# A later place for the router's products, and an earlier one for norms without a partner, in a two-layer graph-attention and mixture-of-experts kernel

## The chip, the cores and the metric

The kernel runs on one core of a Trainium2 chip. A core has a matrix engine (TensorE, PE in the profile, with its weight loads as PEld), a vector engine (VectorE, DVE), a scalar engine (ScalarE, ACT), a general engine (GpSimd, POOL) and an engine that only issues transfers and waits (SyncE, SP). Each takes its own instructions in their written order and waits for others by semaphores. The metric is the device time of one execution in microseconds, the median of several runs.

## The reference

The input x has 64 batches of 256 tokens with 256 features, and a mask of 256 x 256 says which tokens may attend to which. Cut to what matters:

```python
# layer 0
x = x + elu(attention(layernorm(x), adj, W0, a0, heads=4))
x = x + layernorm(x) @ Wf.T + bf
# layer 1
x = x + relu(attention(layernorm(x), adj, W1, a1, heads=1))
t = layernorm(x)                       # 16384 tokens
logits = t @ router.T                  # 8 experts
two best experts per token, weights by softmax over the two
x = x + t + sum over the two: weight * (gelu(t @ w1[e] + b1[e]) @ w2[e] + b2[e])
```

`attention` forms q = h @ W, adds one score per source token and one per target token, applies a leaky relu and the mask, takes a softmax over the targets and multiplies with q. Each batch needs four layer norms: of the input (x0), after the first attention (x1), after the linear layer (x2) and after the second attention (x2 again). Everything is float32.

## The kernel before, in words

**One batch.** `batch_layers` (L506) is a generator that writes the instructions of one batch up to the next `yield`. Its main steps, with the lines that the profile names: the input is turned (L116) and normed, q is projected (L405), scores are spread and masked (L475 on PE, L482 on DVE), the first values are multiplied (L496, 32 products of 65 columns), divided and passed through elu (L503, L534 or L539, L545 to L549); the linear layer (transposes L389, copy L395, products L560, L566 on DVE); the second projection (L440, then L447 to L453 on ACT), second scores (L459, L464) and second values (L496 again, 8 products of 257 columns, reciprocals L503, L582 on ACT, L586 on DVE); the last norm's factors (L591, L594), the normed rows (L600) and the base of the output (L605); and last the router (transposes L389, copy L395, eight small products L630, and a copy of the logits on DVE, L634).

**Norms.** `norm_stats` (L362) takes mean and variance on DVE (L374, L375). The power -1/2 is taken on POOL (L382 adds epsilon, L383 takes the power). To save POOL instructions the power is taken for two norms at once: the first norm of a step is noted in `half_done`, and the second one in the same step calls `finish_norms` (L380) for both. A norm that finds no partner in its step is finished by itself at the end of that step. In full operation two norms meet in each step that has any. Toward the end, when no new batch starts, four of them have no partner: two x1 norms, whose factor L566 uses, and two last norms, whose factor L591 uses.

**Experts.** The tokens of most batches (62 of 64) are sorted by expert. `route` (L939) finds places for the rows of a chunk of batches (the last two chunks have one batch each, the six before them two), and `send` (L920) writes the rows to a buffer `xs` in device memory with indirect DMAs that POOL issues (L922). `expert_pair` (L742) handles 256 rows of one expert: SP loads the rows (L758, L769) and the expert's weights (L784), DVE turns the rows, PE multiplies (L816, gelu on ACT L822, L831), DVE adds a bias (L841), ACT weights them (L809), and `scatter` (L846) adds them to the output with two indirect DMAs from POOL (L852). A scatter waits until the pair of scatters before it has landed, since both may add to the same row. A load of rows waits until the rows sent before it have landed. After the last chunk, SP fills the ends of the experts' regions (L1024), and loads after that wait for it. The last two batches are computed through all experts instead (`dense_expert`, L868).

**Order.** The order is written by a small scheduler (L1090 to L1128). In each step every active generator is advanced once, by rank from low to high; the rank is the number that it yielded last. A new batch starts every third step. So all that is yielded with 35 in a step is written before what is yielded with 40, and so on; sends have 95 and scatters 97. Ranks that matter here: the router's products 35 (L626), the second values 40 (L577), the last norms before the others 60 (L585). Whatever this order says, each engine follows; nothing is reordered later except by waits. PSUM (eight banks) is shared by all these steps, each result taking one bank until it has been read.

The first 16 batches (`EARLY`, L639, `early` at L530) already differ a little: some of their work on DVE is given to ACT and POOL.

The softmax here doesn't subtract the row's maximum and nothing guards it: scores larger than these inputs give would overflow.

## Time and profile before

| | us |
|---|---|
| median of 3 runs | 1607.51 (1606.32 to 1608.09) |
| the profiled execution's own time | 1611.36 |
| its span, first to last instruction | 1609.5 |
| busy: PE | 1468.2 (91%) |
| busy: weight loads | 1299.9 (81%) |
| busy: DVE | 1308.6 (81%) |
| busy: ACT | 860.2 (53%) |
| busy: POOL | 914.6 (57%) |
| mean granted TensorE clock | 0.963 of full speed |

Four stages can be told apart by time. Up to about 320 us there is little expert work yet, and DVE is the busiest (256 of 284 us from 76 to 360). From there to about 1340 us PE is full. From 1340 to 1426 us the last batches pass through and no engine is full. From 1426 to 1552 PE works off the remaining experts, and a chain of scatters follows up to 1609.

In the lines that follow, a group or an instruction is given by time, engine, source line, what is written and read, and in brackets the idle time of its engine before it with what ended that. `rstd` is the factor of a norm, `mv` its mean and variance, `pl` the logits, `pv` the values, `xr` the rows of an expert's pair, `we` its weights.

### The profile page before, as it was taken

The page shows a single profiled execution, that of the slowest core. Times are in us where ns is not written, and L with a number is a line of the kernel's source. Part 1 is how long each engine was busy: PE and PEld are TensorE (multiplying, and loading weights), DVE is VectorE, ACT ScalarE, POOL GpSimd, SP SyncE. Part 2 cuts the span into 40 slices and gives each one's busy share as a digit, 9 for nine tenths or more (in the row PEclk, how much of TensorE's full clock was granted, in tenths as well). Part 3 has the DMA queues.
Part 4 walks back from the last instruction along what each step waited for, and adds up shares of the span by engine and source line. Part 5 has one row for each costly group of instructions (what it writes and reads, how often), then busy time and mean ns, then how long its engine had stood idle before and what let it go on. Part 6 is the DMA issues. An engine that isn't in the chain of part 4 may idle for free.

```text
span 1609.5 us, 30304 instructions
## 1 busy us (share of the span) xinstructions
PE 1468.2 (91%) x8474; PEld 1299.9 (81%) x8474; DVE 1308.6 (81%) x4431; ACT 860.2 (53%) x1968; POOL 914.6 (57%) x875
## 2 busy tenths in 40 slices
PE   7998988999999999999999999999999999489960
PEld 5887777888888888888888888888888887468850
DVE  6898988999898989898989899899899987545530
ACT  2455455465666666556666665555556655343320
POOL 2332636265757576666657575756665567733444
PEclk9999998999999999999999999999999999799985
DMA  5712223466666666665657576664766566787733
GB/s 156 207 50 57 83 74 90 113 152 131 134 145 135 141 143 133 149 145 126 156 119 152 130 155 126 159 129 108 155 129 152 131 120 134 185 174 152 133 47 45
DMA packets 364134, 207.39 MB, mean 129 GB/s; under 512 B 264248, under 2 KB 334912, under 8 KB 363968
## 3 DMA queue, kind: packets, MB, share of 16 engines
q1 hardware_dynamic: 313344, 137.07, 34.7%
q0 software_dynamic: 49632, 67.39, 23.0%
q8 instruction: 70, 1.15, 0.3%
q10 hardware_dynamic: 992, 0.99, 0.2%
q14 instruction: 96, 0.79, 0.2%
HBM read 116.19 MB, written 89.15 MB: 128 GB/s over the span
## 4 chain that ended last, share of the span: by engine, by line
PE 70%; DVE 17%; DMA 3%; ACT 3%; issue 3%; POOL 2%; SPq 1%; DVEq 0%; POOLq 0%; ACTq 0%
PE pv L496 16%; PE ph L816 14%; PE py L831 14%; PE pq L405 6%; PE pq L440 6%; PE pf L560 5%; PE pt L389 4%; DVE z L482 3%; DVE stats L374 2%; PE pl L630 2%; ACT xT L395 2%; DMA out_dram<-y,xt 2%; POOL out_dram L852 1%; DVE mv L375 1%; PE pd L475 1%
## 5 line engine op out<-in xcount | busy, mean ns | idle before, releaser
L852 POOL DMA_INDIRECT out_dram<-y,xt x262 | 417.0, 1592 | 199.7 <-issue 51.1
L496 PE MATMUL pv<-q,z 128*128 128x65 f32 (+1 forms) x2560 | 370.3, 300 | 1.3 <-DVE z L482 1.3
L496 PEld LDWEIGHTS pv<-q,z 128*128 128x128 f32 x2560 | 331.5, 194 | 13.8 <-DVE z L482 1.4
L922 POOL DMA_INDIRECT xs<-xng,pos x248 | 251.2, 1013 | 66.4 <-issue 63.7
L382 POOL TENSOR_SCALAR rstd<-mv 128x4 f32<-128x4 f32 (+1 forms) x132 | 59.3, 449 | 395.5 <-DVE mv L375 347.5
L831 PE MATMUL py<-w2s,hT 128*128 (+1 forms) x1176 | 266.5, 380 | 1.2 <-ACT hT L822 1.2
L395 ACT COPY xT<-pt 128x512 f32<-128x512 f32 x192 | 113.7, 592 | 276.3 <-PE pt L389 276.3
L816 PE MATMUL ph<-sT,we 128*128 128x256 f32 x1048 | 243.6, 386 | 10.0 <-DMA we<-wpack 7.8
L831 PEld LDWEIGHTS py<-w2s,hT 128*128 128x128 f32 x1176 | 219.9, 191 | 30.0 <-ACT hT L822 2.0
L816 PEld LDWEIGHTS ph<-sT,we 128*128 128x128 f32 x1048 | 199.2, 194 | 37.2 <-issue 8.2
L482 DVE SCALAR_TENSOR_TENSOR z<-pd,q,mask 128x256 f32<-128x256 f32 x512 | 211.1, 474 | 0.9 <-PE pd L475 0.9
L822 ACT ACTIVATE hT<-ph,we 128x256 f32<-128x256 f32 x294 | 122.4, 472 | 152.9 <-PE ph L816 130.9
L383 POOL TENSOR_TENSOR rstd<-rstd,mhalf 128x4 f32<-128x4 f32 (+1 forms) x132 | 162.7, 1233 | 11.0
L374 DVE BATCH_NORM_STATS2 stats<-x 128x6 f32<-128x256 f32 x384 | 156.2, 407 | 2.2
L809 ACT ACTIVATE y<-y,w 128x256 f32<-128x256 f32 x262 | 112.4, 501 | 76.0 <-DVE y L841 75.5
L440 PE MATMUL pq<-wx,xT 128*128 128x259 f32 x512 | 130.1, 397 | 18.6 <-ACT xT L395 14.9
L405 PE MATMUL pq<-wx,xT 128*128 128x268 f32 x512 | 133.9, 407 | 5.6 <-DVE xT L116 3.7
L841 DVE TENSOR_TENSOR y<-py,b2s 128x512 f32<-128x512 f32 x131 | 85.9, 685 | 57.9 <-PE py L831 52.6
L440 PEld LDWEIGHTS pq<-wx,xT 128*128 128x128 f32 x512 | 92.5, 190 | 45.2 <-ACT xT L395 29.7
L560 PE MATMUL pf<-wfT,xT 128*128 128x256 f32 x512 | 122.8, 383 | 0.1
L405 PEld LDWEIGHTS pq<-wx,xT 128*128 128x128 f32 x512 | 99.0, 198 | 25.1 <-issue 3.2
L375 DVE BATCH_NORM_AGGREGATE mv<-stats 128x2 f32<-128x6 f32 x512 | 93.1, 182 | 17.5
(156 smaller groups left out, 2262.3 us busy)
## 6 DMA issues: line engine op xcount, KB each, us to landing
we<-wpack SPq DMA_DIRECT2D x139, 288.0 KB
xr<-xs SPq DMA_DIRECT2D x524, 64.0 KB
xblk<-in_x_dram SPq DMA_DIRECT2D x256, 64.0 KB
xin<-in_x_dram SPq DMA_DIRECT2D x64, 256.0 KB
out_dram<-base SPq DMA_DIRECT2D x64, 256.0 KB
out_dram<-y,xt POOLq DMA_INDIRECT x262, 4.1
xs<-xng,pos POOLq DMA_INDIRECT x248, 2.7
xs<-fill SPq DMA_DIRECT2D x9, 260.0 KB
```

The lines of the kernel that those rows point to most:

```text
L374: nc.vector.bn_stats(stats[:, t, :], src[:, t, :])
L383: nc.gpsimd.tensor_tensor(rstd[:, :n], rstd[:, :n], mhalf[:, :n], ALU.pow)
L395: nc.scalar.copy(dst, pt)
L405: nc.tensor.matmul(pq.rearrange("p h c -> p (h c)"), xT[:, k, t * P : (t + 1) * P], wx[:, k, :], start=(k == 0), stop=(k == KT - 1),)
L440: nc.tensor.matmul(pq, xT[:, k, t * P : (t + 1) * P], wx1[:, k, :], start=(k == 0), stop=(k == KT - 1),)
L482: nc.vector.scalar_tensor_tensor(z[:, j, :], pd[:, i, :], q[:, j, h, d + 2 : d + 3], mask[:, j, :], op0=ALU.max, op1=ALU.mult,)
L496: nc.tensor.matmul(pv[:, h, :], z[:, j, t * P : (t + 1) * P], q[:, j, h, : d + 1], start=(j == 0), stop=(j == NT - 1),)
L560: nc.tensor.matmul(pf[:, t, :], xT[:, k, t * P : (t + 1) * P], wfT[:, k, :], start=(k == 0), stop=(k == KT - 1),)
L816: nc.tensor.matmul(ph[:, f, :], we[:, k * D + f * P : k * D + (f + 1) * P], xT[:, k, :], start=(k == 0), stop=(k == KT - 1),)
L831: nc.tensor.matmul(py[:, t, :], hT[:, f, t * P : (t + 1) * P], w2s[:, e, f * D : (f + 1) * D].rearrange("p e c -> p (e c)"), start=(f == 0 ...
L852: d = nc.gpsimd.indirect_dma_start(out=out_rows, out_offset=bass.IndirectOffsetOnAxis(ap=xt[:, t, 0:1].bitcast(I32), axis=0), in_=y[:, t, ...
L922: d = nc.gpsimd.indirect_dma_start(out=xs_d[: E * CAP * PAIR, :], out_offset=bass.IndirectOffsetOnAxis(ap=at, axis=0), in_=xe, in_offset=None,
```

## The change

Two edits in the order; no instruction is added or taken away.

```diff
@@ batch_layers
         xT = transposed(xe[:, :, :D], *(("xTd", DENSE) if dense else ()), blocks=True)
-        yield 35
+        yield 45 if early else 35
         pl = bank("pl", [NT, E])
@@ the scheduler's step
             while queue:
                 *_, entry = heapq.heappop(queue)
+                if half_done and entry[0] > 75:
+                    finish_norms(NT)
                 entry[0] = next(entry[2], None)
```

The first edit gives the router's products of batches 0 to 15 the rank 45, so that they are written behind the second values of another batch (rank 40) where they stood ahead of them. On PE the eight L630 products change places with eight L496 products of 257 columns; on DVE the copy of the logits (L634) goes behind two reciprocals (L503). The banks of the three results change hands accordingly: the second half of the next first projection (L405), which took the router's bank before and does so after, waits for the copy of the logits either way.

The second edit finishes a norm that has no partner before the first entry of a rank above 75 in its step, and no longer at the step's end. Where nothing of such a rank is issued by POOL in that step, the order on POOL stays. It changes in four places, all toward the end: the norms at 1318.3, 1343.4, 1373.2 and 1397.9 us of the profile. The first two move ahead of two sends and two scatters, the third ahead of two sends and two scatters, the fourth ahead of two scatters. All other instructions of POOL keep their order, and so do those of ACT and SP.

## The prediction

> **What bounds the kernel now.** I read the stages first (busy time by stretch of time: length, then busy us of PE, weight loads, DVE, ACT, POOL, then granted clock, DMA share, GB/s).

> ```profile
> 1240.00:1300.00 60.00, 59.52 (x351) 53.48 (x350) 54.70 (x200) 34.50 (x75) 36.03 (x33) 1.00 0.59 122
> 1340.00:1375.00 35.00, 24.78 (x117) 20.38 (x115) 20.07 (x108) 13.71 (x31) 25.36 (x24) 0.90 0.68 125
> 1375.00:1400.00 25.00, 14.10 (x64) 12.25 (x64) 13.55 (x75) 10.36 (x21) 16.95 (x16) 0.77 0.67 134
> 1400.00:1426.00 26.00, 15.51 (x61) 12.63 (x61) 17.40 (x75) 11.78 (x25) 13.32 (x11) 0.76 0.87 219
> 1426.00:1552.00 126.00, 124.82 (x568) 108.90 (x569) 61.08 (x146) 49.84 (x113) 52.46 (x34) 0.99 0.71 135
> ```

> The long middle (320 to 1340 us) is full on PE and the change doesn't touch its order. From 1340 to 1426 nothing is full: that stage is a chain of waits, and half of the change lies there. The other half lies before about 345 us (batches 0 to 15), where DVE is busy over 90% of the time.

> In the tail I read who DVE waits for (1300 to 1426 us; total, times, longest), then SP's DMA queue (1340 to 1430):

> ```profile
> DVE by L591 <- POOL rstd L383: 18.1, 3, 10.1
> DVE x L566 <- POOL rstd L383: 9.0, 2, 6.4
> ```
> ```profile
> SPq L758 <- DMA xs<-xng,pos: 25.6, 3, 13.0
> ```

> Four norms without a partner hold DVE for 2.60, 6.38, 7.81 and 10.11 us, 26.9 in sum. But SP, which issues the loads that the last experts need, is held by something else: sent rows that must land. POOL in order of time shows why:

> ```profile
> 1340.42 1.61 POOL L852 DMA_INDIRECT out_dram<-y,xt  x1 [0.35 <-issue]
> 1342.34 1.57 POOL L852 DMA_INDIRECT out_dram<-y,xt  x1 [0.30 <-ACT hT L822]
> 1343.38 0.82 POOL L382 TENSOR_SCALAR rstd<-mv 128x2 f32<-128x2 f32 x1
> ...
> 1347.09 0.23 POOL L382 TENSOR_SCALAR rstd<-mv 128x4 f32<-128x4 f32 x1 [2.07 <-DVE tail L679]
> 1347.40 1.02 POOL L383 TENSOR_TENSOR rstd<-rstd,mhalf 128x4 f32<-128x4 f32 x1
> 1348.61 1.62 POOL L852 DMA_INDIRECT out_dram<-y,xt  x1 [0.19 <-issue]
> ...
> 1370.27 1.60 POOL L852 DMA_INDIRECT out_dram<-y,xt  x1 [1.54 <-issue]
> ...
> 1385.43 1.00 POOL L922 DMA_INDIRECT xs<-xng,pos  x1 [0.30 <-issue]
> ```
> ```profile
> 1388.19 1.98 SPq L758 DMA_DIRECT2D xr<-xs  x4
> ...
> 1400.13 7.00 SPq L1024 DMA_DIRECT2D xs<-fill  x8
> 1412.45 1.92 SPq L758 DMA_DIRECT2D xr<-xs  x4
> ```

> The send at 1385.43 plus 2.7 us (median of the sends to landing here) is 1388.1, and there SP's 13.0 us wait ends. From then on SP issues without a pause, except 5.0 us for the landing of the fill, until the weight loads at 1422, whose landing starts PE's last full stretch at 1425.87; that one ends at 1552, and a chain of scatters follows to the end. So the tail's path is POOL, then SP, and not the engine with the longest waits.

> **The change part by part.** The sum is made against the profiled execution, 1611.36 us (span 1609.5), and the difference is put on the median 1607.51, which is 3.85 lower.

> *Norm A (was 1318.3 to 1319.9).* It comes ahead of the sends at 1312.55. Its statistics were complete at 1310.25, so it doesn't stand. A lone norm costs POOL 1.1 us (scatter's end 1343.91 to rstd's end 1345.0), so two sends and two scatters go 1.1 later, the scatters' end to 1319.9. DVE's wait of 2.60 goes, the next paired norm's statistics are there at 1319.3 instead of 1321.9, and that norm (1.3 to 2.1 us) ends by 1322.0 instead of 1324.2. What follows on POOL is 2.2 earlier.

> *Norm B (was 1343.9 to 1345.0).* Its statistics were complete at 1329.4. With A's shift the scatter that ended at 1337.40 ends at 1335.2; B adds 1.1, so sends and scatters behind it are 1.1 earlier and end at 1342.8. DVE's 6.38 goes: it reaches L566 at 1338.7, the next paired norm no longer waits until 1347.09 but runs 1342.8 to 1344.2. What is late next is the scatter of 1348.61: it must wait until the scatter before has landed. Seven such gaps between 1308 and 1396 (end of one pair to start of the next) are 3.05 to 4.67, mean 3.65. 1342.8 + 3.65 = 1346.5: 2.1 earlier (ends 2.7 and 1.1). The scatters of 1356.14, 1362.67 and 1370.27 each waited for that landing already (4.02, 3.05, 4.15), so the 2.1 is handed on unchanged.

> *Norm C (was 1373.7 to 1374.8).* It goes ahead of the sends at 1366.42, which fit: they end 1.3 later, at 1370.0, inside the idle 1.54 before 1370.27. It leaves the line between the scatter's end at 1373.73 and the send at 1375.01: 1.28. Now 3.4 earlier, through the serial run of sends and scatters to the send of 1385.43, hence SP's loads and the last PE stretch. DVE's 7.81 mostly goes; its cover is that SP waits for the sends anyway.

> *Norm D (was 1397.9 to 1399.6).* It goes ahead of a scatter pair that waits 4.67 for landing, where it costs nothing. The four sends behind come 1.3 earlier, but SP's load of 1412.45 waits for the fill, not for them. 10.11 us of DVE's wait goes for nothing.

> SP itself and its waits keep their order. On POOL no instruction is added; the four norms only change places. Tail: 3.4 us gain.

> *Router behind the second values, 16 batches.* Eight products (0.96 to 1.06 us) go behind eight of L496 (1.84). PE stood before the router in 7 batches, for 8.2 us together, the longest

> ```profile
> 178.81 1.06 PE L630 MATMUL pl<-rT,xT 128*128 128x8 f32 x8 [2.34 <-ACT xT L395]
> 252.31 1.88 PE L630 MATMUL pl<-rT,xT 128*128 128x8 f32 x8 [2.26 <-ACT xT L395]
> ```

> and the values, ready long before (z ended at 248.7 in the second), now fill it. But who is paid? DVE carries the chain from 145 to 320, and of its waits there

> ```profile
> DVE rinv L503 <- PE pv L496: 3.5, 3, 1.6
> DVE x L566 <- PE pf L560: 0.7, 3, 0.3
> ```

> two of 1.6 follow PE's wait in the routing (L956), which stays. What the swap can end is 0.33 at 257.85 and 0.16 at 95.94: 0.5 us. Upper bound: all DVE waits for PE from 76 to 330 us, 5.6. Lower: DVE's copy of the logits comes after two reciprocals (0.22 for both), and the second half of the next L405 products takes its bank: 16 x 0.22 = 3.5 lost if PE always stood there; it stood at L405 for DVE's reciprocal once, 1.3. I take 0.5, as PE has slack in that stage.

> In that wait the granted clock fell: 1.00 in 248 to 252, 0.52 in 252 to 256, and eight L496 products took 3.77 instead of 1.98. [...]

> [...] The row: the power took 0.72 with DVE idle, 1.52 at 1322.68 with DVE busy. By that A and B cost 0.8 more each, and the tail would gain 1.8 instead of 3.4.

> Sum: 3.4 + 0.5 = 3.9. 1607.5 - 3.9 = **1603.6 us**.

> **The rivals.**
> *B, POOL gives it back.* The sends wait behind the norms (1.1 each for A and B), the power is slow beside DVE, and the paired norms come no earlier on POOL because sends and scatters are ahead of them. For: POOL is serial from 1366 to 1388. Against: paired norms are late through DVE's wait. Only C's 1.28 and part of 0.5 remain: about 1606.
> *C, more goes through.* DVE, ACT and PE run ahead, base stores clear sooner, and four landings (after 1342.8, 1352, 1359.6, 1366) all take the shortest, 3.05: 0.6 + 1.0 + 1.1 = 2.7 more, 6.6 in all: 1600.9.
> *D, slower.* The same four landings lengthen, because loads and base stores now bunch with them: their forecast sum is 14.9; at 4.7 each (seen once: 4.67) the gain is gone, at 6.0 each it is 24.0, a loss of 9.1 - 3.9 = 5.2: 1612.7. It decides above 4.7 mean. Against: DMA's share is already 0.67 in these windows and the mean was 3.65.

> **How the numbers follow.** 0.2%, 3.2 us, is about what a measurement of this kernel tells from no change. Forecast 0.50, own range 2.6 to 5.5 gain (1602.0 to 1604.9), of which 0.36 counts as faster and 0.14 as same, since 3.9 stands just past the bound; B 0.22, same; C 0.15, faster; D 0.13, slower. Faster 0.51, same 0.36, slower 0.13. Range: from a little below C, 1600, to 1609, short of D; some 0.18 lies outside.

> **What would show it.** Right: DVE's waits for lone rstd gone (under 4 us of 26.9 left); the scatter of 1348.61 at about 1346.5; SP's load of 1388.19 at about 1385; PE's last full stretch from about 1422.5, unchanged in length; PE's waits before the router under 2 us, with DVE's end of the early stage within 1 us. Wrong: SP's load at 1388 or later (B, D); landing gaps above 4.7 (D); SP waiting for something other than sends, or the early stage 3 us or more shorter, since then PE carried it and not DVE.

## The result: slower by 0.4%, and the profile after

The changed kernel took 1612.48 us (median of 7 runs, 1611.37 to 1614.87) where the kernel before, run beside it, took 1606.32 (7 runs, 1602.15 to 1608.09). The ratio is 1.0039, with a 95% interval from 1.0026 to 1.0051: 6.2 us slower, between 4.2 and 8.2. I had forecast 3.9 us faster, with 1609.0 as the upper end.

The two profiled executions differ by much less, 1612.47 against 1611.36 us, because the profile of before happens to lie above all timed runs of before. To see where time went, I set each instruction of DVE against the same instruction of the other profile. In the first 60 us, where nothing is changed, the changed kernel came out 3.7 us ahead by chance. From 60 to 370 us it lost 5.4 us. From there to 1290 us the distance kept within 0.3 us. From 1290 to 1500 us it gained 0.6. The loss came in three jumps: about 1.5 us at 140 us, 2.4 at 287 and 1.4 at 326; the first two stand behind a routing. So the loss lies in the early stage, where edit 1 (the router) is, and the gain of edit 2 (the norms) is small.

What DVE waits for PE in the early stage, 76 to 330 us, in the profile after (total, times, longest):

```profile
DVE rinv L503 <- PE pv L496: 6.7, 5, 1.6
DVE z L464 <- PE pd L459: 2.3, 3, 0.8
```

Before, the same two rows had 3.5 (shown in the prediction) and 0.8. That is 4.7 us more of waiting on the engine that carries this stage. Why PE was late is seen in PE's own waits in that stretch, first before:

```profile
PE pp L956 <- DVE m L948: 8.5, 3, 3.7
PE pl L630 <- ACT xT L395: 8.2, 7, 2.3
```

and after:

```profile
PE pp L956 <- DVE m L948: 14.0, 3, 5.4
PE pl L630 <- ACT xT L395: 2.8, 4, 0.8
```

The two rows add up to 16.7 us before and 16.8 after. The edit did end most of PE's waits at the router, as forecast, but the idle time wasn't removed. It went to the next place where PE has to wait for DVE: the routing products (L956). PE's other waits over 0.15 us in that stretch even rose, from 4.4 to 8.8 us in all, as the whole stage got longer. The routing products come once per chunk of four batches and need `m`, DVE's last step of choosing the two experts.

What that does is seen at the third routing. Before, with a wait of 2.05 us, the eight products of L405 that follow take 2.03 us:

```profile
281.22 0.41 PE L956 MATMUL pp<-m,tri 128*128 128x64 f32 x2 [2.05 <-DVE m L948]
281.46 0.39 PE L957 MATMUL pp<-m,ones 128*128 128x64 f32 x2
281.69 2.03 PE L405 MATMUL pq<-wx,xT 128*128 128x268 f32 x8
```

After, with a wait of 5.36 us, the same products take nearly double:

```profile
279.04 0.66 PE L956 MATMUL pp<-m,tri 128*128 128x64 f32 x2 [5.36 <-DVE m L948]
279.49 0.64 PE L957 MATMUL pp<-m,ones 128*128 128x64 f32 x2
279.92 3.89 PE L405 MATMUL pq<-wx,xT 128*128 128x268 f32 x8
```

The stages by time tell why (the last three numbers of each line are granted clock, DMA share and GB/s). Before:

```profile
276.00:280.00 4.00, 3.00 (x17) 2.23 (x15) 3.75 (x12) 3.19 (x9) 3.28 (x4) 0.99 0.20 71
280.00:284.00 4.00, 2.78 (x17) 2.47 (x18) 3.82 (x14) 2.73 (x7) 1.01 (x1) 1.00 0.29 104
```

and after:

```profile
276.00:280.00 4.00, 0.96 (x5) 0.99 (x5) 3.69 (x16) 2.94 (x8) 2.04 (x3) 0.62 0.24 86
280.00:284.00 4.00, 4.00 (x13) 3.02 (x12) 3.31 (x14) 0.00 (x0) 1.28 (x3) 0.52 0.45 103
```

A second place has nothing to do with routing. The second projection (L440) at 314 us waits in both kernels for the same step of DVE. Before and after:

```profile
313.82 1.99 PE L440 MATMUL pq<-wx,xT 128*128 128x259 f32 x8 [1.82 <-DVE by L594]
```
```profile
313.98 3.27 PE L440 MATMUL pq<-wx,xT 128*128 128x259 f32 x8 [1.88 <-DVE by L594]
```

The wait is the same but for 0.06 us, yet the products take 1.3 us longer (the granted clock was 1.00 from 312 to 320 us before, and 0.82 and 0.76 in the two halves of that stretch after), and DVE waits 1.32 us at 327 us where it waited under 0.4 before.

In the tail DVE's waits for norms fell, from 26.9 us to 13.3, not to the 4 that I had named (profile after, 1300 to 1426 us):

```profile
DVE by L591 <- POOL rstd L383: 12.9, 4, 6.3
...
DVE x L566 <- POOL rstd L383: 0.4, 1, 0.4
```

and SP's queue shows no gain, as the tail was entered 1.4 us later and gained about 0.9 by here:

```profile
1388.71 1.93 SPq L758 DMA_DIRECT2D xr<-xs  x4
1400.34 7.15 SPq L1024 DMA_DIRECT2D xs<-fill  x8
1413.50 1.92 SPq L758 DMA_DIRECT2D xr<-xs  x4
```

### The profile page after: what moved, and what is told of

Read it like the earlier page. It is cut to its first block, busy times and chain, and to the rows that moved or that the text cites. A ratio compares the mean times of both kernels' runs of the same rounds, so it can differ in the third digit from the quotient of the medians.

```text
span 1610.7 us, 30301 instructions
## 1 busy us (share of the span) xinstructions
PE 1463.4 (91%) x8474; PEld 1296.6 (81%) x8474; DVE 1310.2 (81%) x4431; ACT 859.1 (53%) x1968; POOL 914.3 (57%) x875
## 5 line engine op out<-in xcount | busy, mean ns | idle before, releaser
L852 POOL DMA_INDIRECT out_dram<-y,xt x262 | 416.5, 1590 | 201.7 <-issue 47.8
L496 PE MATMUL pv<-q,z 128*128 128x65 f32 (+1 forms) x2560 | 367.1, 298 | 3.0 <-DVE z L482 3.0
L496 PEld LDWEIGHTS pv<-q,z 128*128 128x128 f32 x2560 | 330.8, 193 | 15.6 <-DVE z L482 3.6
L922 POOL DMA_INDIRECT xs<-xng,pos x248 | 251.4, 1014 | 66.6 <-issue 64.1
L382 POOL TENSOR_SCALAR rstd<-mv 128x4 f32<-128x4 f32 (+1 forms) x132 | 60.7, 460 | 396.6 <-DVE mv L375 352.1
L395 ACT COPY xT<-pt 128x512 f32<-128x512 f32 x192 | 113.6, 591 | 259.0 <-PE pt L389 258.8
L822 ACT ACTIVATE hT<-ph,we 128x256 f32<-128x256 f32 x294 | 122.4, 470 | 157.7 <-PE ph L816 134.6
L383 POOL TENSOR_TENSOR rstd<-rstd,mhalf 128x4 f32<-128x4 f32 (+1 forms) x132 | 162.7, 1233 | 11.0
L809 ACT ACTIVATE y<-y,w 128x256 f32<-128x256 f32 x262 | 112.4, 501 | 85.6 <-DVE y L841 85.1
L440 PE MATMUL pq<-wx,xT 128*128 128x259 f32 x512 | 130.3, 397 | 19.8 <-ACT xT L395 16.0
L405 PE MATMUL pq<-wx,xT 128*128 128x268 f32 x512 | 133.5, 406 | 5.5 <-DVE xT L116 3.2
L841 DVE TENSOR_TENSOR y<-py,b2s 128x512 f32<-128x512 f32 x131 | 85.9, 686 | 57.6 <-PE py L831 53.1
L440 PEld LDWEIGHTS pq<-wx,xT 128*128 128x128 f32 x512 | 92.7, 191 | 46.4 <-ACT xT L395 30.7
L560 PE MATMUL pf<-wfT,xT 128*128 128x256 f32 x512 | 122.4, 383 | 0.1
L405 PEld LDWEIGHTS pq<-wx,xT 128*128 128x128 f32 x512 | 98.7, 197 | 25.7 <-issue 3.6
```

The lines of the kernel that those rows point to most:

```text
L383: nc.gpsimd.tensor_tensor(rstd[:, :n], rstd[:, :n], mhalf[:, :n], ALU.pow)
L405: nc.tensor.matmul(pq.rearrange("p h c -> p (h c)"), xT[:, k, t * P : (t + 1) * P], wx[:, k, :], start=(k == 0), stop=(k == KT - 1),)
L440: nc.tensor.matmul(pq, xT[:, k, t * P : (t + 1) * P], wx1[:, k, :], start=(k == 0), stop=(k == KT - 1),)
L496: nc.tensor.matmul(pv[:, h, :], z[:, j, t * P : (t + 1) * P], q[:, j, h, : d + 1], start=(j == 0), stop=(j == NT - 1),)
L560: nc.tensor.matmul(pf[:, t, :], xT[:, k, t * P : (t + 1) * P], wfT[:, k, :], start=(k == 0), stop=(k == KT - 1),)
L822: nc.scalar.activation(hT[:, f, :], ph[:, f, :], AF.Gelu, bias=we[:, C_B1 + f : C_B1 + f + 1])
```

## Experiments

Theory T1: edit 1 is the loss, through the clock, and edit 2 gains a little. Rivals: T2, edit 2 loses in the tail; T3, both lose; T4, edit 1 loses by its order (the logits' copy behind the reciprocals, the hand-over of PSUM banks) and the clock only shows it. Each ratio below is to the kernel before on the same chip; its median there was 1608.35, 1605.88 and 1610.10 us in the three sets.

### Each edit alone

Edit 1 alone:

```diff
-        yield 35
+        yield 45 if early else 35
         pl = bank("pl", [NT, E])
```

> Edit 1 alone (router behind the second values in batches 0 to 15; norms as before). Theory T1: edit 1 is the loss. PE no longer waits before the router, so its idle time collects in the one wait before the routing products (L956: 2.74, 3.72 and 2.05 us before; 3.32, 5.36 and 5.36 in the changed kernel), the granted clock is at half behind it, and the products that DVE needs next are late: DVE's waits for PE behind the three routings and at 327 us rose from 4.0 to 9.0 us. T1 expects 5 to 6 us slower than before, 1611 to 1613. Theory T2: edit 2 is the loss, in the tail; then this kernel stands within 1 us of before, 1605.5 to 1607. Theory T3: both cost a part; about 1609.

Measured: ratio 1.0036 (1.0021 to 1.0050), 5.8 us slower (3.4 to 8.0). The three waits before L956 were 3.33, 5.36 and 5.36 us again.

Edit 2 alone:

```diff
                 *_, entry = heapq.heappop(queue)
+                if half_done and entry[0] > 75:
+                    finish_norms(NT)
```

> Edit 2 alone (norms without a partner finished ahead; router as before). T1 expects 0.5 to 1 us faster than before, since the shift between the two profiles goes from +1.44 us at 1300 us to +0.88 at the end: 1605.3 to 1606. My prediction's own sum for this part was 3.4 faster: 1603. T2 expects 5 us slower, 1611. T3 about 1609.

Measured: ratio 0.9997 (0.9981 to 1.0012), between 3.1 us faster and 1.9 us slower. T2 falls, and of T3 no more than 1.9 us is left: edit 1 alone is enough for the loss. What edit 2 is worth isn't settled by this run.

### The wait filled with work that nobody reads

Products into the bank that the routing products overwrite afterwards; they need nothing that PE waits for. In the changed kernel:

```diff
-        pp = bank("pp", [2, E, nt])
+        whole_bank = bank("pp", [2 * D])
+        for _ in range({0: 5, 1: 9, 2: 9}.get(c, 0)):
+            nc.tensor.matmul(whole_bank[:, :N], tri, masks[0][:, 0, :], start=True, stop=True)
+        pp = whole_bank[:, : 2 * E * nt].rearrange("p (a b c) -> p a b c", a=2, b=E)
```

> The changed kernel, and in the wait before the routing products of the first three routings PE computes 5, 9 and 9 products of 128x256 that nobody reads (about 2.4, 4.4 and 4.4 us at full clock, inside the waits of 3.32, 5.36 and 5.36). T1 (it is the clock that falls in that wait): DVE's waits of 0.83, 0.53, 1.61, 0.83, 1.60, 0.64 and 1.60 us behind the routings go, 4 to 7.6 us faster than the changed kernel, 1605 to 1608.5, with the first L405 products behind the routing at 2.0 us instead of 3.89. Rival T4 (the loss comes from the order of the logits' copy on DVE and the hand-over of PSUM banks, and the clock only shows it): no gain, 1612 to 1613, or slower if the filler delays the routing products.

Measured: ratio 0.9980 (0.9963 to 0.9997), 3.2 us faster than before where the changed kernel was 6.2 slower. At the third routing, in time order on PE:

```profile
273.44 4.05 PE L957 MATMUL pp<-mask,tri 128*128 128x256 f32 x18
278.89 0.43 PE L959 MATMUL pp<-m,tri 128*128 128x64 f32 x2 [1.39 <-DVE m L948]
279.16 0.39 PE L960 MATMUL pp<-m,ones 128*128 128x64 f32 x2
279.38 2.03 PE L405 MATMUL pq<-wx,xT 128*128 128x268 f32 x8
```

(Line numbers stand three higher here, so L959 is L956.) The eighteen products, nine in the program, fill the wait, L405 takes 2.03 us, and DVE's waits of 9.0 us in the two rows of the early stage are down to 1.6. Work added to PE, which nobody uses, makes the kernel 8 to 9 us faster than edit 1 alone, run beside it: the loss was the clock (0.52 granted, and L405 at 3.89 us, behind this wait in the changed kernel). T4 can't explain this. The gain is more than the 6.2 us that the change lost: the kernel before had slow products behind its first two routings as well (L405 at 3.17 and 3.89 us), and edit 2 is in this kernel too. The 1.6 that is left stands behind the one place that wasn't filled, L440:

```profile
311.55 3.79 PE L440 MATMUL pq<-wx,xT 128*128 128x259 f32 x8 [1.87 <-DVE by L594]
```

The kernel before with two of its waits filled:

```diff
+        for _ in range({0: 4, 1: 6}.get(c, 0)):
```

> The kernel before, with 4 and 6 such products (about 1.9 and 2.9 us) in the waits before the routing products of the first two routings (2.74 and 3.72 us). T1: DVE's waits behind these two (1.60; 0.82 and 1.60) go, up to 4.0 us faster than before, 1602.3 to 1605. T4: no change, 1606.

Measured: ratio 0.9993 (0.9975 to 1.0011), 1.1 us faster with no change inside the interval. The profile shows L405 at 2.02 and 2.03 us behind both routings, as expected, but the gain that I expected isn't shown by the times. (DVE's rows gained 3.9 us on those of before between 60 and 370 us in the one profiled execution; the interval of the times reaches to 4.0 us faster.)

### The router's order with the routing waits filled in both

Edit 2 and three filled waits, without edit 1; it differs from the filled changed kernel in edit 1 (and in how much filling each order has room for):

```diff
+                if half_done and entry[0] > 75:
+                    finish_norms(NT)
...
+        for _ in range({0: 4, 1: 6, 2: 3}.get(c, 0)):
```

> The kernel before with edit 2 and with 4, 6 and 3 products of 128x256 that nobody reads in the waits before the first three routing products (2.74, 3.72 and 2.05 us). Set beside the changed kernel with its three waits filled, it differs in edit 1 alone, with the clock kept up behind the routing in both. T1 (edit 1 costs only through the clock): the two agree within 2 us, this one 1604 to 1608. T4 (edit 1 costs by its order too): this one is 2 to 5 us faster than the changed kernel with its waits filled, 1600 to 1603.

Measured: ratio 0.9974 (0.9962 to 0.9985), 4.2 us faster than before. That is 0.0006 below the filled changed kernel, 1 us, well inside the two intervals. The products aren't equally fast everywhere, though: at L440 near 310 us the filled changed kernel still takes 3.79 us (line above) and this one 1.99, and by DVE's rows the former lost 2.7 us from 290 to 330 us, this one nothing. So no loss is seen that the order itself would have to explain. This ratio is the lowest up to here, but its interval overlaps that of the filled changed kernel. A second time, in a later set of runs:

> The kernel before with edit 2 and the first three routing waits filled with 4, 6 and 3 products, a second time, on the same chip as the kernel that differs from it in edit 2 alone. As in its first runs: about 4 us faster than before. Against the kernel with the three waits filled and without edit 2 it shows what edit 2 is worth when the clock's losses behind the routings are out of the way: by the time from the third scatter behind 1284 us to the scatter at 1421 us in the traces so far (127.4, 125.9, 127.0 us with edit 2; 128.5, 128.8, 128.3 without) 1.7 us faster; by my prediction's sum 3.4 faster; by rival B of the prediction 1.3 to 1.5 faster; by rival D slower.

Measured: ratio 0.9964 (0.9947 to 0.9982), 5.8 us faster. And the same without edit 2:

```diff
+        for _ in range({0: 4, 1: 6, 2: 3}.get(c, 0)):
```

> The kernel before with the first three routing waits filled with 4, 6 and 3 products, without either edit. T1: behind the three routings L405 takes 2.0 us and DVE no longer waits 1.6 us for the first values; 2 to 4 us faster than before, and 1.7 us slower than the same kernel with edit 2.

Measured: ratio 0.9990 (0.9976 to 1.0005), 1.6 us faster, under the 2 to 4 that I expected. The difference of the two, 0.0026 or 4.2 us (3.2 by the medians), is edit 2 in a kernel whose L405 takes 2.02 or 2.03 us behind all three routings; the two intervals overlap. Edit 2 alone had shown 0.5. I come back to this below.

### Transposes in place of products

So far the filler was products. Whether transposes do the same in a wait has a bearing on what can fill it, and on PE's many transposes here.

```diff
+        for _ in range({0: 16, 1: 30, 2: 30}.get(c, 0)):
+            nc.tensor.transpose(whole_bank[:, :P], masks[0][:, 0, :P], ident)
```

> The changed kernel with the waits before the first three routing products filled as before, but with 16, 30 and 30 transposes of 128x128 that nobody reads, in place of 5, 9 and 9 products of 128x256 (by the L475 row, 0.60 us for 4, again about 2.4, 4.4 and 4.4 us). If transposes keep the granted clock up as products do: like the kernel filled with products, 1603 to 1608, and L405 behind the routing at 2.0 us. [...]

Measured: ratio 1.0005 (0.9992 to 1.0019), between the kernel filled with products (0.9980) and the changed one (1.0039). The transposes took less time than I had reckoned (0.115 us each), so 1.58, 1.70 and 2.02 us were left idle, and L405 took 2.02, 3.35 and 2.92 us. This doesn't decide, so the number was raised to leave as little idle as the products did:

```diff
+        for _ in range({0: 21, 1: 38, 2: 40}.get(c, 0)):
```

> The changed kernel with 21, 38 and 40 transposes in the three routing waits: at 0.115 us each, as measured (30 took 3.44 us), they leave about 1.1, 0.8 and 0.9 us idle, as the 5, 9 and 9 products did, where the 16, 30 and 30 left 1.58, 1.70 and 2.02. If transposes keep the clock up as products do: L405 takes 2.0 us behind all three routings and the time is that of the kernel filled with products, 0.2 to 0.3% under before. If they don't count: L405 takes 2.9 to 3.9 us behind some of them, whatever the idle time left, and the time is before's or more.

Measured: ratio 0.9976 (0.9962 to 0.9990), 3.9 us faster than before. At the second and third routing:

```profile
200.85 4.31 PE L957 MATMUL pp<-ident,mask 128*128 128x128 f32 x38
205.05 0.43 PE L959 MATMUL pp<-m,tri 128*128 128x64 f32 x2
205.32 0.39 PE L960 MATMUL pp<-m,ones 128*128 128x64 f32 x2
205.55 2.03 PE L405 MATMUL pq<-wx,xT 128*128 128x268 f32 x8
```
```profile
278.06 0.43 PE L959 MATMUL pp<-m,tri 128*128 128x64 f32 x2 [0.93 <-DVE least L666]
278.33 0.39 PE L960 MATMUL pp<-m,ones 128*128 128x64 f32 x2
278.55 2.02 PE L405 MATMUL pq<-wx,xT 128*128 128x268 f32 x8
```

Behind all three routings L405 took 2.02 or 2.03 us, as it did behind the products: float32 transposes of 128x128, back to back, can stand in for products here, with 1.03 us left idle at the first routing and 0.93 at the third. Whether they can where more is left idle isn't shown: with 1.70 us left idle behind 30 of them L405 took 3.35 us, and no wait behind products fell between 1.51 and 1.98 us.

### Which batches make the wait grow

Edit 1 without the last batch of each chunk, and in the last batch alone:

```diff
+        yield 45 if early and b % 4 != 3 else 35
```

> Edit 1 alone, and not in the last batch of a chunk (batches 3, 7, 11, 15), so that the order of the products right ahead of a routing is that of the kernel before. If the wait before the routing grows because PE loses nothing in the batches ahead (waits before the router, slow products behind them), the waits before L956 are those of the changed kernel less the 0.8 us or so that the last batch's router waits: over 4 us at the second and third routing, and the time is 1611 to 1613 as with edit 1 whole. If it grows because of the order in the last batch itself, the waits are as before (2.7, 3.7, 2.1) and the time is 1606 to 1608.

```diff
+        yield 45 if early and b % 4 == 3 else 35
```

> Edit 1 alone, and only in the last batch of each of the first four chunks (3, 7, 11, 15), the complement of the run without them. There the waits at the second and third routing were 3.75 and 3.65 us, with edit 1 whole 5.36 and 5.36, without it 3.72 and 2.05. If the two parts add up, the order in the last batch alone gives 3.72 + 1.61 = 5.3 and 2.05 + 1.71 = 3.8 us, L405 at half clock behind the second and mostly behind the third, and about half of edit 1's loss: 2 to 3 us slower than before. If they don't, the waits stay under 4 us and the time within 1 us of before.

Measured: 1.0009 (0.9994 to 1.0024) without the last batch, 1.0025 (1.0008 to 1.0041) with the last alone. The two excesses add up to 0.0034, against 0.0036 for edit 1 alone. At the third routing, without the last batch and with it alone:

```profile
275.74 0.66 PE L956 MATMUL pp<-m,tri 128*128 128x64 f32 x2 [3.65 <-DVE m L948]
276.62 3.89 PE L405 MATMUL pq<-wx,xT 128*128 128x268 f32 x8
```
```profile
277.54 0.66 PE L956 MATMUL pp<-m,tri 128*128 128x64 f32 x2 [5.36 <-DVE ohs L668]
278.42 3.67 PE L405 MATMUL pq<-wx,xT 128*128 128x268 f32 x8
```

Neither expectation was fully met. Without the last batch the waits at the second and third routing were 3.75 and 3.65 us, not over 4; with it alone 4.98 and 5.36 us, where adding up would have given 5.3 and 3.8. The waits don't add, but both parts lengthen them: the third wait was 2.05 us before, and each part alone took it well past 3. For the last batch the order gives a reason: eight L496 products (1.98 us) no longer come between its router and the routing. At the third routing the wait grew by 3.3 us, more than that, so it isn't the whole of it. How the batches ahead do it was not taken apart further.

### Is PE on the path at the end?

```diff
         ph = bank("ph", [KT, PAIR])
+        calls.append(0)
+        if len(calls) > PAIRS + FLUSH - 16:
+            for _ in range(2):
+                nc.tensor.matmul(ph[:, 0, :], tri, masks[0][:, 0, :], start=True, stop=True)
```

> The kernel before, and in the last 18 expert jobs PE first computes two products of 128x256 that nobody reads (18 x 2 x 0.49 us = 17.6 us more on PE, between about 1450 and 1552 us). My prediction had SP's loads and then PE's last full stretch on the path to the end: by that the end comes 17 us later, 1625. The other reading, from the profile: each pair of scatters waits for the landing of the pair before, and its rows were ready 15 to 45 us earlier in the whole tail (36 us and more in the last 20 pairs), so the chain of scatters alone sets the end: no change, 1604 to 1610.

Measured: ratio 1.0011 (0.9993 to 1.0028), 1.8 us slower with no change inside the interval, and far from 17. PE was busy for 140.3 us from 1426 to 1580 us, 13.4 more than in the kernel before. Its last lines, and POOL's last scatter (this kernel's line numbers stand six higher):

```profile
1562.13 1.89 PE L822 MATMUL ph<-sT,we 128*128 128x256 f32 x8
1563.86 3.62 PE L837 MATMUL py<-w2s,hT 128*128 x16
```
```profile
1600.16 1.54 POOL L858 DMA_INDIRECT out_dram<-y,xt  x1 [0.30 <-issue]
```

In the kernel before, PE and DVE were done at 1555 us, 13 us sooner, and the last scatter left no sooner, at 1601.55. DVE's last line and POOL's last scatters there:

```profile
1554.15 0.69 DVE L841 TENSOR_TENSOR y<-py,b2s 128x512 f32<-128x512 f32 x1 [1.04 <-PE py L831]
```
```profile
1593.25 1.54 POOL L852 DMA_INDIRECT out_dram<-y,xt  x1 [3.04 <-DMA out_dram<-y,xt]
1595.09 1.54 POOL L852 DMA_INDIRECT out_dram<-y,xt  x1 [0.30 <-issue]
1599.71 1.54 POOL L852 DMA_INDIRECT out_dram<-y,xt  x1 [3.07 <-DMA out_dram<-y,xt]
1601.55 1.54 POOL L852 DMA_INDIRECT out_dram<-y,xt  x1 [0.30 <-issue]
```

A pair of scatters takes 6.45 us, of which some 3.75 us are the landing that the next pair waits for. The rows of the last pair were ready at 1555.8, when ACT had weighted them (L809), and left at 1599.7. I measured this distance (end of L809 to start of the scatter) for the last 44 pairs of before: never under 14 us, and 34 us or more in the last 19. With the longer PE it is still 21 us or more in the last 19. So the end is set by the chain of scatters alone: this run shows it for the stretch in which PE got its added work, and the distances say the same from 1430 us on, where POOL issues nothing else.

## Why the prediction was wrong

**The router: the step that failed.** "What the swap can end is 0.33 at 257.85 and 0.16 at 95.94: 0.5 us" counted what the edit ends, and "PE has slack in that stage" excused the rest. The true term is a loss: DVE's rows of the two profiles with edit 1 whole lost 5.4 and 4.1 us between 60 and 370 us against the profile of before, three without it lost 0, -0.8 and -0.7; about 5.2 us in the mean, and 5.8 by the times. This is also beyond my lower bound of 3.5, which was built from the copy of the logits. That copy moved by 0.2 us in a batch, and DVE was back in step right behind it.

Of PE's wait in the routing (L956) the prediction said that it "stays". It grew from 8.5 to 14.0 us, and that is the mechanism it had wrong. What was missing is the question that I asked of POOL and not of PE: a stall goes, so what is late next? PE's pace in that stage is set by DVE, so its idle time doesn't go away (16.7 us in the two rows before, 16.8 after). Here, filling holes ahead of a wait that DVE ends made that wait longer. Many short waits, of which most cost nothing, became long ones right ahead of products that DVE needs, and two of the three long ones cost more than before. The third part of the loss, about 1.4 us, isn't of this kind: at L440 the wait stayed the same, and only the products behind it became slow. I had the row: the granted clock at 0.52 behind a wait of 2.26 us, and L496 at 3.77 us for 1.98. I didn't ask what it says of a wait that grows.

**The tail: the size about right, the way there wrong.** Seven profiles have edit 2 and seven have not (before and after among them). What else differs between these kernels lies before 370 us, or, with the longer PE, at the very end. So I set the tails against each other, one pair of scatters after the other. Mean time from the pair before, in us:

| pair of (time in before) | without | with | sum of differences |
|---|---|---|---|
| 1308.79 | 8.74 | 8.94 | +0.4 |
| 1315.37 | 6.70 | 7.60 | +1.3 |
| 1327.08 | 11.79 | 8.43 | -2.1 |
| 1333.91 | 7.09 | 8.48 | -0.7 |
| 1340.42 | 6.70 | 7.68 | +0.3 |
| 1348.61 | 8.19 | 7.33 | -0.6 |
| 1380.24 | 9.98 | 9.18 | -1.7 |
| 1404.99 | 9.99 | 9.08 | -2.8 |
| 1413.73 | 8.87 | 9.74 | -1.9 |
| the last | 6.41 | 6.42 | -2.6 |

(The sum runs over all pairs from that of 1299.91 on; of the rows, those that the four norms touch are shown, and the last.)

- Norm A, 1.1 later and then 2.2 earlier: right up to the pair of 1327.08 (+0.9, then -3.4). Wrong right behind it: 1.4 us went back, because the landing that releases the next pair took longer. In the profile after:

```profile
1326.51 1.62 POOL L852 DMA_INDIRECT out_dram<-y,xt  x1 [0.30 <-issue]
1328.44 1.57 POOL L852 DMA_INDIRECT out_dram<-y,xt  x1 [0.30 <-issue]
...
1335.78 1.60 POOL L852 DMA_INDIRECT out_dram<-y,xt  x1 [3.17 <-ACT y L809]
```

  The row names `y`, but `y` had been ready for more than 20 us; the trace has the scatter of 1328.44 landing at 1334.93, 6.5 us after its start, and the next pair leaves 0.85 us after that. In before the same scatter landed in 4.1 us, and the next pair left 0.85 us after it too. From the end of one pair to the start of the next this is 5.77 us for 3.35. Rival D needed a mean above 4.7 at four other places, ahead of the pairs of 1348.61 to 1370.27; there the profile after has 3.58, 3.28, 3.06 and 3.99, 13.9 in sum, less than the 14.9 of the forecast.
- Norm B, 2.1 earlier at 1348.61: it cost 1.0 in front (forecast 1.1) and gave 0.9 behind, nothing in sum.
- Norm C, 1.28: it gave 0.8. Norm D, nothing: it gave 0.9 and lost it at the next pair, as forecast.
- The price of 0.8 us each that the prediction set on A and B for running beside a busy DVE didn't show, and its two rows can't give it: 0.72 is the power for one norm (128x2), 1.52 for two (128x4). With two L841 running on DVE all the while, norm A's power took 0.72 in the profile after. For two norms it took 1.02 at 1347.40 in before, beside a DVE that was busy for 87% of it. The second line here is the 1.52 of before:

```profile
1314.25 0.72 POOL L383 TENSOR_TENSOR rstd<-rstd,mhalf 128x2 f32<-128x2 f32 x1
```
```profile
1322.68 1.52 POOL L383 TENSOR_TENSOR rstd<-rstd,mhalf 128x4 f32<-128x4 f32 x1
```

- "The tail's path is POOL, then SP" and PE's last stretch: wrong. SP's loads came 0.9 us earlier by the profile after, when the later start is taken off, and PE's last stretch isn't on the path at all. The chain of waits led me through PE because a scatter's row names the rows' last writer; the distance between "ready" and "sent" would have told me. What reaches the end is what POOL's chain of scatters gains.

Together edit 2 gained 2.6 us by these profiles (from the pair of 1292.22 to the end: 314.5 us in the mean with it, 311.1 to 318.7; 317.1 without, 315.4 to 319.9), 4.2 by the pair of filled kernels, 0.5 (between 3.1 faster and 1.9 slower) alone. Forecast was 3.4. The sign is a gain where it shows at all; its size stays open between about 0.5 and 4 us. Edit 1 at +5.8 and edit 2 at -0.5 give 5.3, and the two together measured 6.2 (4.2 to 8.2).

**The rivals.** D's time, 1612.7, was the measured one, but by chance: its mechanism didn't occur at its four places. None of my rivals made the router the loss, and the one bound that let it lose (3.5 us) priced another mechanism, so the range ended at 1609.0.

**The signs to look for.** PE's waits before the router "under 2 us": 2.8. DVE's end of the early stage "within 1 us": it came 5.4 us later, and the warning "SP's load at 1388 or later" came true at 1388.71. The scatter of 1348.61, forecast for about 1346.5, left at 1350.43.

## What to carry to other kernels

When an engine's pace is set by another, closing its short waits may shorten nothing, as here (16.7 us before, 16.8 after): add up its waits before and after and expect no smaller sum, then ask where the sum will stand and what runs right behind it. On PE one long wait was worse here than short ones, because what followed it ran at about half the clock (0.52 granted, L405 at 3.89 us for 2.03) and was on the path; a few products that nobody reads, placed in the wait, were worth more than the new order. At the end of a kernel, measure for each last transfer how long its data had been ready before believing that the engine which made them is on the path.

## What the runs showed of the clock

The first three routings of twelve profiles (those with transposes left out) give 36 waits before L956 and the time of the eight L405 products behind each. I call 2.02 to 2.03 us full: at the third routing of before, with 2.03 us, the granted clock was 1.00 from 280 to 284 us.

| wait | L405 behind it |
|---|---|
| 0 to 1.5 us (15 waits, 14 of them cut short by products that nobody reads) | 2.02 or 2.03 in all |
| 2.0 to 3.1 us (9) | full in 5; 2.77 to 3.28 in 4 |
| 3.3 to 5.4 us (12) | 2.99 to 3.89 in all |

In these profiles the length of the wait alone didn't settle it: behind waits of 2.73 and 2.74 us L405 was full in one execution and slow in two (3.17 and 2.77 us). All twelve waits of 3.3 us and more had slow products behind them, and the shortest wait that had was 1.98 us, with L405 at 3.28.

The table holds for the routing alone. Elsewhere a shorter wait was followed by slow products too, as ahead of a router in the kernel before (these eight L496 products take 1.98 us at 309.14 us, where the granted clock was 1.00; here it was 0.83 from 270 to 274 us and 0.74 from 274 to 278):

```profile
271.09 1.06 PE L630 MATMUL pl<-rT,xT 128*128 128x8 f32 x8 [1.07 <-ACT xT L395]
272.01 3.18 PE L496 MATMUL pv<-q,z 128*128 128x257 f32 x8
```

A difference went with what stood ahead of the wait, too. At L440 near 310 us the wait was 1.82 or 1.83 us in all eight kernels that leave batch 13's router ahead of the second values, and L440 took 1.99 us in all eight. With the eight router products of 8 columns right ahead of the two groups of transposes and the wait, it was 1.87 or 1.88 us in five kernels, and L440 took 2.53 to 3.79 us in all five. In the sixth (38 and 40 transposes) the wait was broken in two, 0.24 and 0.50 us, and the products took 1.14 and 1.11 us for four each. Whether the eight short products ahead are the cause isn't shown: I made no run for it alone.
